# Nine blocks at a time for the narrow products of a layer: a group size in a graph kernel's last stage

## The chip, the cores and the metric

The kernel runs on one core of a Trainium2 chip. The metric is device time in microseconds: three runs of the kernel before took 556.18, 557.09 and 557.86 us, so its time is the median, 557.09.

## The reference

Four graph layers run one after another over x (3327 nodes of 64 features) with one dense matrix adj, whose entries are zero or positive. After each layer comes x = layernorm(x + layer(x)). Only the last layer matters here, and of it this core:

```python
support = input @ weight
mask = (adj != 0).astype(support.dtype)
rank = jnp.cumsum(mask, axis=1)
deg = rank[:, -1:]
k = jnp.minimum(deg, float(MAX_NEIGH))        # MAX_NEIGH = 100
pos = rank - (deg - k)
w = mask * jnp.where(pos > 0, DECAY ** (k - pos), 0.0)   # DECAY = 0.5
out = w @ support + bias
```

For every node, its neighbours are counted from the last column back. The last neighbour has weight 1, the one before it 1/2, and so on, up to a hundred of them. The output is the weighted sum of the neighbours' support rows.

## The kernel before

The matrix comes transposed and padded to 3328 = 26 blocks of 128 rows (`NB`), in HBM as `in_adjT`; a block's rows are the neighbours and its columns the nodes. Layer 1 goes through it once, layer 2 twice, and layer 3 once more. Everything in layer 3 is in `layers`, from line 523 on.

Layer 3 splits the nodes into two halves of 1664 columns (`HALF`) and each half into two chunks (c = 0 and 1) of 832, which a matmul covers in two pieces (e = 0 and 1) of 416 (`CW`). A half goes through the 26 blocks from the last to the first, so there are 52 steps. For each step:

- `masks(q)`, line 324: the half block `ah` is loaded by a DMA on SyncE's queue (832 KB; the first four blocks of each half are in SBUF already, as `kept`), and VectorE turns it into a bf16 `mask` of zeros and ones (L341). There are four `ah` buffers and six masks. It is called with q + 3 (`AHEAD`).
- `advance(c, q)`, line 544: TensorE adds to the counts in PSUM (`cnt`, one accumulator for each chunk) with `count` (L526): first what is left of block q (matrix `rest`), then the running count within block q + 1 (matrix `tri`). The counts are prepared so that their integer value is the bit pattern of a bf16 weight: a larger count is a smaller power of two.
- `read(c, q)`, line 531: the counts are clamped at zero and written as int16 into a weight tile `w`, which is then used as bf16. ScalarE reads chunk 0 (L541), and VectorE chunk 1 (L539). A chunk's next counts overwrite the accumulator, so they wait for this.
- `products(q, c)`, line 714: TensorE multiplies the weights by the support rows. The support in fp32 is kept as three bf16 parts. The first two stand side by side in `s12`, 128 columns wide, and are multiplied at once (`high`, L722) into an accumulator `acc` of 128 partitions. The third part, `s3`, has 64 columns only; its products (L737) go into one half of the accumulator's partitions, the lower for e = 0 and the upper for e = 1.

The wide products of a step follow when its weights are there, three steps later (`LEAD`). The narrow ones are put on a list and are done for several blocks at once:

```python
later.append((q, c))
if not last:
    high(q, c)
if last or c and len(later) == 2 * GROUP:
    for ql, cl in later:
        if last and cl != c:
            continue
        for e in range(2):
            nc.tensor.matmul(acc[h, cl][e * D : (e + 1) * D, e, :], s3[...], ws[ql, cl][:, e, :], ...)
```

`last` is the last block of a half: there each chunk's list is emptied before its last wide product. So a weight tile must live until its group is through, and `read` takes it from a pool whose depth follows from the group:

```python
w = l3w.tile([P, 2, CW], BF16, tag=f"w{c}", bufs=LEAD + GROUP + 2, ...)
```

The order of instructions on TensorE, VectorE and ScalarE is written out by hand: what the program says is the order of the queue. The loop is this:

```python
for q in range(LEAD, len(steps) + LEAD + 1):
    turn = q == NB + LEAD
    read(0, q, False)
    if turn: first_out = half_out(0, sums_out(0))
    read(1, q, True)
    if with_step: with_step.pop(0)()
    masks(q + AHEAD)
    p = q - LEAD if q < NB + LEAD else q - LEAD - 1
    for c in range(2):
        if p and not turn: products(p, c)
        if q < len(steps): advance(c, q)
        ...
```

So in a step's TensorE queue stand: wide products of chunk 0, counts of chunk 0, wide products of chunk 1, then the group of narrow ones if it is due, then the counts of chunk 1. `with_step` holds nine pieces of work left from the start of the layer (making the parts of the support, L644 to L653, and scaling rows for later, L626), one for each of the steps q = 3 to 11; some are VectorE's, some ScalarE's and GpSimd's. `half_out` is the output of the first half: a bias (L752 on ScalarE, L753 on VectorE), 13 small products that bring it back to rows (L759), the sum with x (L794), squares (L795), their sums (L798), a reciprocal square root (L239 to L246 and L555), the scaling (L803) and two stores. It is drawn out over the steps q = 29 to 34. After the loop `last_out` does the same for the second half.

Of the kernel before, what the change touches and what calls it, by code (L numbers as in the profile page):

```python
# [63 lines left out]
CUBIC_PLUS = 2 * CUBIC_ROOT - 1  # L64
CUBIC_REST = 1.75705840270866
NEIGH = 100
GROUP = 3
LEAD = 3
AHEAD = 3
STEP = float(2**7)  # L70
# [6 lines left out]
def kernel(  # L77
# [234 lines left out]
    def layers(ctx, x2, x3, begun_here, kept, ready, ahead_ctx, strm):  # L312
# [218 lines left out]
        def read(c, q, vector):  # L531
            if q >= len(steps):
                return
            h, jb = steps[q]
            w = l3w.tile(
                [P, 2, CW], BF16, tag=f"w{c}", bufs=LEAD + GROUP + 2, name=f"w_{h}_{jb}_{c}"
            )
# [176 lines left out]
        def products(q, c):  # L714
# [5 lines left out]
            def high(q, c):  # L720
                for e in range(2):
                    nc.tensor.matmul(  # L722
                        acc[h, c][:, e, :], s12[:, slot(jb)].rearrange("p t d -> p (t d)"),
                        ws[q, c][:, e, :], start=first, stop=last,
                    )
# [4 lines left out]
# [4 lines that stand above are left out]
# [1138 lines left out]
```

## Time and profile before

| | |
|---|---|
| median of three runs | 557.09 us |
| the profiled execution, its time | 557.54 us |
| its span, first to last instruction | 555.7 us |
| TensorE (PE) busy | 527.5 us, 95% |
| VectorE (DVE) busy | 372.2 us, 67% |
| ScalarE (ACT) busy | 276.8 us, 50% |
| GpSimd (POOL) busy | 207.4 us, 37% |
| mean granted TensorE clock | 0.979, and 1.00 in layer 3's loop |
| L526, counts, 408 matmuls 128 x 128 x 416 | 339 to 340 ns each |
| L722, wide products, 208 matmuls 128 x 128 x 416 | 339 ns each |
| L737, narrow products, 208 matmuls 128 x 64 x 416 | 344 ns each, 22.1 us busy |
| L539, VectorE's read of counts, 49 | 1023 ns each |
| L541, ScalarE's read of counts, 55 | 863 ns each |
| L341, masks from `ah`, 42 | 1034 ns each |
| `ah` loads, 832 KB each, 42 | 6.3 us from issue to landing |

A matmul's length in the table is that from its start to its end; matmuls overlap, and what counts is how far apart they start. "Idle before" is time in which an engine stood still ahead of an instruction, with the one that ended it behind the arrow; "issue" means that nothing in the profile explains it. The busy share of TensorE is an average over layers with different limits, so the prediction cuts the span into stretches. In layer 3's loop the profile is best read step by step, by the starts of instructions on the timeline.

### The profile page before, as it was taken

To read this page: it belongs to the slowest core of one execution; us is meant where nothing else is said; L and a number is where in the kernel's file an instruction comes from. 1 tells how busy PE (TensorE), PEld (TensorE's weight loads), DVE (VectorE), ACT (ScalarE), POOL (GpSimd) and SP (SyncE) were. 2 spreads that over 40 slices of the span, in tenths; PEclk is the share of its full clock that TensorE was granted. 3 is DMA by queue.
4 is the path that set the end of the run, shared out by engine and by line. 5 is a ranking of instruction groups with operands and counts; after the bars stand their busy time and mean duration, and the time that the engine had idled before them with its cause. 6 is when DMAs were issued, how large, how long until landed. Compare 5 with 4: busy or idle time off the path is not lost.

```text
span 555.7 us, 7392 instructions
## 1 busy us (share of the span) xinstructions
PE 527.5 (95%) x2841; PEld 226.9 (41%) x2841; DVE 372.2 (67%) x549; ACT 276.8 (50%) x325; POOL 207.4 (37%) x85
## 2 busy tenths in 40 slices
PE   8799989999999999999999999999999999999991
PEld 5422222222222222964444444434455555545541
DVE  6799999999999999798000011200678877887733
ACT  4899999999999997620000100000464333433321
POOL 3699999999999999000000000000001000000000
PEclk9889999999999999799999999999999999999996
DMA  8958866666667536799998049999029994799601
GB/s 282 365 205 288 257 209 225 210 223 220 225 232 243 187 123 247 277 416 425 423 427 367 1 163 424 426 426 399 6 66 344 329 326 167 246 296 349 247 1 38
DMA packets 33893, 143.57 MB, mean 258 GB/s; under 512 B 10269, under 2 KB 11959, under 8 KB 28855
## 3 DMA queue, kind: packets, MB, share of 16 engines
q1 hardware_dynamic: 31511, 142.40, 69.7%
q10 hardware_dynamic: 2336, 0.59, 0.5%
q8 instruction: 24, 0.39, 0.3%
q14 instruction: 22, 0.18, 0.1%
HBM read 141.53 MB, written 0.87 MB: 256 GB/s over the span
## 4 chain that ended last, share of the span: by engine, by line
PE 68%; DVE 17%; issue 7%; ACT 6%; POOL 1%; DVEq 0%; POOLq 0%; ACTq 0%
PE cnt L421 26%; PE cnt L526 11%; DVE v L1124 10%; PE pq L1103 9%; PE acc L722 6%; PE acc L1136 4%; PE acc L737 3%; ACT pq L1116 3%; ACT sg L1076 2%; DVE a L1115 2%; DVE w L539 1%; PE cnt L412 1%; DVE mask L341 1%; PE idle L928 1%; PE x_w L1455 1%
## 5 line engine op out<-in xcount | busy, mean ns | idle before, releaser
L1088 POOL TENSOR_TENSOR sg<-sg,at 128x1664 f32<-128x1664 f32 x44 | 163.7, 3738 | 3.7 <-ACT sg L1076 2.2
L1103 PE MATMUL pq<-riT,ljT 64*128 64x416 f32 x416 | 101.0, 564 | 11.6 <-DVE v L1124 7.9
L1116 ACT ACTIVATE pq<-pq,al,ga 128x832 f32<-128x832 f32 x104 | 104.6, 1012 | 12.1 <-DVE a L1115 12.0
L1115 DVE SCALAR_TENSOR_TENSOR a<-pq,sg 128x832 f32<-128x832 f32 x104 | 105.3, 1013 | 4.5 <-PE pq L1103 2.3
L1124 DVE SCALAR_TENSOR_TENSOR v<-pq,a 128x832 f32<-128x832 f32 x104 | 105.4, 1014 | 3.3 <-ACT pq L1116 2.2
L1136 PE MATMUL acc<-v,xv 128*64 128x416 f32 x416 | 96.0, 541 | 0.0
L1076 ACT ACTIVATE sg<-lb,rb 128x1664 f32<-128x1664 f32 (+1 forms) x53 | 87.3, 1649 | 0.0
L541 ACT ACTIVATE w<-cnt 128x832 int16<-128x832 f32 x55 | 47.3, 863 | 71.5 <-PE cnt L526 71.4
L421 PE MATMUL cnt<-at_l,lj 128*64 128x416 f32 x448 | 80.4, 513 | 0.0
L653 POOL TENSOR_TENSOR s<-sq,s 128x384 bf16<-128x384 f32 (+1 forms) x4 | 4.1, 1026 | 200.7 <-ACT s L652 200.7
L506 ACT ACTIVATE x<-cnt 128x416 f32<-128x416 f32 x8 | 4.1, 518 | 131.5 <-PE cnt L421 131.5
L539 DVE TENSOR_SCALAR w<-cnt 128x832 int16<-128x832 f32 x49 | 50.1, 1023 | 25.8 <-PE cnt L526 24.0
L1103 PEld LDWEIGHTS pq<-riT,ljT 64*128 64x128 f32 x416 | 31.7, 186 | 85.1 <-DVE v L1124 78.6
L526 PE MATMUL cnt<-mask,tri 128*128 128x416 bf16 x208 | 53.5, 339 | 0.1
L722 PE MATMUL acc<-w,s 128*128 128x416 bf16 x208 | 52.6, 339 | 0.5 <-DVE hid L794 0.5
L526 PE MATMUL cnt<-mask,rest 128*128 128x416 bf16 x200 | 51.6, 340 | 1.2 <-ACT w L541 0.6
L421 PEld LDWEIGHTS cnt<-at_l,lj 128*64 128x64 f32 x448 | 31.9, 137 | 46.2 <-issue 45.4
L1136 PEld LDWEIGHTS acc<-v,xv 128*64 128x64 f32 x416 | 20.7, 135 | 61.5 <-issue 57.8
L409 DVE COPY lj<-pn_l 128x512 f32<-128x512 f32 (+1 forms) x4 | 2.4, 592 | 61.6 <-PE pn_l L373 61.6
L341 DVE TENSOR_SCALAR mask<-ah 128x1664 bf16<-128x1664 f32 x42 | 43.4, 1034 | 0.0
L421 PE MATMUL cnt<-kept,lj 128*64 128x416 f32 x224 | 41.2, 513 | 0.0
L586 DVE TENSOR_TENSOR x<-x,xc 128x416 f32<-128x416 f32 x4 | 2.4, 588 | 41.5 <-ACT x L506 41.5
(285 smaller groups left out, 441.9 us busy)
## 6 DMA issues: line engine op xcount, KB each, us to landing
at_l<-in_adjT SPq DMA_DIRECT2D x24, 1664.0 KB, 12.8
at<-in_adjT SPq DMA_DIRECT2D x44, 832.0 KB, 4.9
ah<-in_adjT SPq DMA_DIRECT2D x42, 832.0 KB, 6.3
bt_l<-in_adjT SPq DMA_DIRECT2D x8, 1664.0 KB, 14.9
kept<-in_adjT SPq DMA_DIRECT2D x7, 1664.0 KB, 8.1
lb<-lf_rows SPq DMA_DIRECT2D x2, 384.0 KB, 6.1
ljT<-ljT SPq DMA_DIRECT2D x4, 128.0 KB, 5.5
x<-in_x ACTq DMA_DIRECT2D x1, 416.0 KB, 5.4
```

Source lines behind the costliest of these rows:

```text
L341: nc.vector.tensor_scalar(mask[q], at, 0.0, None, ALU.not_equal)
L421: nc.tensor.matmul(acc[c][h * D : (h + 1) * D, :], hw[:, slot(jb), :], blocks[jb][:, o : o + CW], start=c not in begun, stop=last, skip_gr ...
L526: nc.tensor.matmul(cnt[c][:, e, :], mat, mask[q][:, of], start=start, stop=(mat is tri), skip_group_check=True,)
L539: nc.vector.tensor_scalar(w.bitcast(I16), cnt[c], 0.0, None, ALU.max)
L722: nc.tensor.matmul(acc[h, c][:, e, :], s12[:, slot(jb)].rearrange("p t d -> p (t d)"), ws[q, c][:, e, :], start=first, stop=last,)
L1076: nc.scalar.activation(sg[:, :, of], lbs[:, :, of], AF.Sigmoid, bias=rb[:, sl : sl + 1])
L1088: nc.gpsimd.tensor_tensor(sg[:, :, of], sg[:, :, of], at[:, :, of], ALU.mult)
L1103: nc.tensor.matmul(pq[:, h, :], ljT[h != jb // NBH][rows, of], riT[rows, ch * CW : (ch + 1) * CW], start=True, stop=True,)
L1115: stt(a_s[t], pqs[t], CUBIC_PLUS, us.pop(t), op0=ALU.add, op1=ALU.mult)
L1116: nc.scalar.activation(pqs[t], pqs[t], AF.Square, bias=al[:, one], scale=ga[:, one])
L1124: stt(w, pqs.pop(t), CUBIC_REST, a_s.pop(t), op0=ALU.add, op1=ALU.mult)
L1136: nc.tensor.matmul(accs[cp, ci][h * D : (h + 1) * D, :], xv[:, slot(jb), :], w[:, h, :], start=(jb == orders[cp][0]), stop=(jb == orders[c ...
```

## The change

The group size of the narrow products goes from three blocks to nine.

```diff
-GROUP = 3
+GROUP = 9
 LEAD = 3
 AHEAD = 3
```

By `len(later) == 2 * GROUP` the narrow products are now taken up after nine blocks, 36 matmuls in a row where there were 12. In each half of 26 blocks the groups end after the 9th and the 18th block, and the other eight blocks stand at the half's end, 16 matmuls for each chunk, ahead of its last wide product. By `bufs=LEAD + GROUP + 2` each chunk's pool of weight tiles has 14 buffers where it had 8. No other line of the kernel changes; the number of instructions on every engine stays the same.

## The prediction

> **What bounds the kernel now.** The change touches layer 3 alone, so I first cut the span: layer 3 runs from the first counting matmul at 397.6 us to the end at 555.7. The chain that ended last gives the whole:
>
> ```profile
> PE 68%; DVE 17%; issue 7%; ACT 6%; POOL 1%; DVEq 0%; POOLq 0%; ACTq 0%
> ```
>
> Shares of the span cannot say which engine decides in which step, so I read the timeline of TensorE over an undisturbed stretch. Columns: start, length, engine and line, shapes, count.
>
> ```profile
> 445.38 0.52 PE L526 MATMUL cnt<-mask,rest 128*128 128x416 bf16 x2
> 445.74 0.52 PE L526 MATMUL cnt<-mask,tri 128*128 128x416 bf16 x2
> 446.09 0.52 PE L722 MATMUL acc<-w,s 128*128 128x416 bf16 x2
> 446.53 1.25 PE L737 MATMUL acc<-w,s 128*64 128x416 bf16 x12
> 447.71 0.53 PE L526 MATMUL cnt<-mask,rest 128*128 128x416 bf16 x2
> ```
>
> Full-width pairs start 0.352 us apart (0.176 a matmul), with no gap. A step is six such pairs, 2.11 us. The third part (L737, 64 columns wide) comes in groups of twelve matmuls; groups start 7.61 us apart here (438.92, 446.53), which leaves 7.61 - 3 x 2.11 = 1.28 us for a group. Its twelve matmuls run as six concurrent pairs, 6 x 0.176 = 1.06, so **0.22 us a group is neither**: 0.09 lost on the way in (446.53 where 446.44 was due), the rest on the way out. The view of line 737 shows where it sits, and how many groups there are: the weight loads stand idle in front of it 20 times, 6.9 us, by "issue".
>
> The same stretch on VectorE:
>
> ```profile
> 443.12 1.02 DVE L539 TENSOR_SCALAR w<-cnt 128x832 int16<-128x832 f32 x1 [0.15 <-PE cnt L526]
> 444.06 1.02 DVE L341 TENSOR_SCALAR mask<-ah 128x1664 bf16<-128x1664 f32 x1
> 445.23 1.02 DVE L539 TENSOR_SCALAR w<-cnt 128x832 int16<-128x832 f32 x1 [0.15 <-PE cnt L526]
> ```
>
> A step without a group costs it 0.94 + 1.02 = 1.96 us, of 2.11: **0.15 us to spare**. A group gives it 1.28 more. Where VectorE has other work it decides. The chain in order of time (start, length, what) through the output of the first half shows it:
>
> ```profile
> 484.26 1.02 DVE mask L341
> 485.28 0.20 DVE v_out L798
> 485.48 0.31 issue
> 485.79 0.48 DVE v_out L798
> 486.27 0.93 DVE w L539
> 487.20 0.93 DVE mask L341
> 488.14 0.09 DVE v_out L555
> ...
> 490.51 0.93 DVE mask L341
> 491.44 0.60 DVE hid L803
> 492.04 0.94 DVE w L539
> 492.99 0.04 issue
> 493.03 0.86 PE cnt L526 x4
> ```
>
> From 484.26 to 493.03 no matmul is on it, though TensorE's timeline has a group of L737 at 486.74: that group is free today.
>
> **What the Trainium skill says.** "TensorEngine Tiling (Array Packing)", Tiling Modes: changing the tiling mode drains TensorE, and column tiles work in parallel. The trace agrees on both: 0.22 us a group, and twelve narrow matmuls in the time of six. "TensorE: Matmul & The Clock Gate", Architectural detail, calls VectorE's queue strict FIFO: a late mask holds the read of counts behind it. "SBUF — State Buffer", two separate sides: a VectorE operation in a two-port mode and GpSimd exclude each other. Here the mask at 411.18, begun beside GpSimd's L653 (411.10, 0.91 us), took 1.72 us against 1.02.
>
> **The change, part by part.** No instruction is added or dropped; the build of the changed kernel keeps every engine's count, and orders TensorE anew. q is the loop's step, p the block multiplied: p = q - 3 in the first half, q - 4 in the second.
>
> 1. *Switches saved.* Before, each half has groups after p = 2, 5, ..., 23 of that half, and two at its end (one for each column chunk): 10, and 20 in all as seen. After: p = 8, 17 and the two at the end: 4, and 8. Twelve fewer, 12 x 0.225 = **-2.70 us**. The 208 narrow matmuls themselves only move: a group taken out brings all behind it 1.28 forward, and 1.06 of it comes back in a later group. That holds where TensorE decides; below, each place that loses a group is priced by the stall it leaves.
>
> 2. *First steps, q = 5 to 10.* VectorE has other work here (L648 0.55 and 0.68; L626 0.55 and 0.68), and the groups at q = 5 and 8 go. At q = 6, VectorE's order (read 414.78, L648, mask 416.19) puts the next read at 417.14 and its end at 418.16; matmuls need it at 418.10 and hear of it 0.05 later: 0.11 late. At q = 8 the L648 of 0.68 gives, by the same sum, a read that ends at 424.72 for a matmul due at 424.54: 0.23. L626 at q = 10 and 11 falls under the group that stays at q = 11. Together **+0.34**. GpSimd's L653 can stretch a mask once: 0 to +0.7, taken as nothing, since the masks then start near its end.
>
> 3. *q = 26.* The first block of the second half has no "rest" pairs, so its step is 0.70 shorter and VectorE is behind: a stall of 0.23 today (467.04 where 466.81 was due), and a second one when the group at 468.88 is gone: VectorE's read starts at 467.83 straight behind a mask and is heard of at 467.83 + 1.02 + 0.05 = 468.90, the matmuls are due at 468.44 + 0.35 = 468.79: **+0.11**.
>
> 4. *Output of the first half, q = 30 to 34.* Without the group at q = 32 the matmuls would be due at 486.65, but the read ends at 487.21; then ScalarE's read waits behind the square root (488.25), which waits for VectorE, and at q = 33 the matmuls start at 490.56, as today. The 1.28 us saved are lost whole. At q = 35 the matmuls are due at 495.13 and the read ends at 495.25, seen at 495.30: 0.17. Together **+1.45**. From there VectorE has no other work.
>
> 5. *Loads of the adjacency, between groups.* SyncE issues a load when the mask four earlier has ended. Between groups that leaves 4 x 2.11 - 1.02 = 7.42 us to land, where today a group or two lies between (8.7 or more). Landing took 4.7 to 10.9 us, median 6.3; around 506 to 516 us:
>
> ```profile
> DMA to landing us min/median/max: 6.3/7.6/7.9
> ```
>
> Loads issued less than four steps ahead of a group, or under it, land in its shadow (3.4 us). Left are the last four of each eight-step run, q = 16 to 19 and 43 to 46. With today's times only the second run is late, by 7.9 - 7.4 = 0.5; rate makes it worse: a load of 832 KB (851,968 bytes) each 2.11 us asks 404 GB/s, where 498 to 505.6 us moved 369, one load each 2.31, with the DMA engines at share 1.00. Bounds: 0, and 1.6: if each of four loads adds 0.2 to the queue, the second run is 1.3 late, and 0.3 is kept for the first (6.6 us at most around 440). I take **+0.50**, what today's times give. Queued behind a late mask: VectorE's next read, and TensorE behind that.
>
> 6. *The tail.* The last products of the second chunk become eight blocks in place of two, so ScalarE's L752 (540.41, 0.96 us) ends under them; L759 starts behind the last product, 541.13, and not at 541.42: **-0.29**.
>
> 7. *Nothing:* the twelve buffers, six for each chunk (1664 bytes a partition each). They move addresses: the first mask load waits for VectorE and TensorE instead of a DMA and TensorE, with 27 us in hand (issued 377.17, used 411.18). A read finds its buffer free two steps early (14 deep, oldest released after p = 8, needed at p = 14). In a 3.4 us group ScalarE and VectorE run dry, but the next counts need only reads that are already done.
>
> Sum: -2.70 - 0.29 + 0.34 + 0.11 + 1.45 + 0.50 = -0.59. The profiled execution took 557.54 us (span 555.7 and 1.8 around it), 0.45 above the median of 557.09; the sum goes on the median: **556.5 us**.
>
> **The rivals.**
> - *TensorE decides throughout, faster:* items 1 and 6 with 2 and 3 only, -2.54: 554.6. It needs VectorE to catch up in the output steps, as it does after 495 us. Against: the chain above. Partial forms (loads never late, 0.3 less in item 4) reach 555.7.
> - *Masks starve, slower:* loads are served no faster than today's average, one each 2.54 us. Then each of the two long runs loses 8 x (2.54 - 2.11) less about 1.0 of slack, 2.4; two are 4.8 in place of 0.5: 560.8. It decides from landing times of 7.4 us on; the two runs must lose 2.8 for a slowdown past 0.3%. For it: 7.6 around 511 us. Against: 369 GB/s were reached, and there is no VectorE wait on a load today.
> - *The change does nothing:* the groups would stay short. The build's order shows TensorE without L737 until nine blocks are through, so this is open only if a long group's switches cost 2.5 times a short one's; that undoes item 1: +2.1, 559.2.
>
> **How the numbers follow.** About 0.3% (1.7 us) is what a measurement can tell from none. Balance 0.63 (own range 555.6 to 558.0), faster 0.20, slower 0.17, the last with the unpriced waits in it. The range 554.8 to 558.7 leaves a tenth out on each side.
>
> **What would show it.** Right: eight groups of L737, full ones of 36 matmuls in about 3.4 us; "issue" idle of its loads near 2.7; a chain through VectorE from q = 31 to 35; L759 right behind the last product. Wrong: VectorE idle by a load of ah, or masks over 1.1 us; TensorE stalls at q = 12 to 20 or 39 to 46; a group costing other than 0.22 beyond its pairs.

## The result, and the profile after

The changed kernel takes 555.70 us (median of 20 runs) against 557.24 of the kernel before (20 runs), a ratio of 0.9976 (95% interval 0.9967 to 0.9985): 0.8 to 1.8 us shorter. The middle of that, 1.3 us, is within the 0.3% that the prediction called no difference, on the side that it forecast.

A whole run scatters by more than the pieces discussed here; what is ahead of layer 3 is the same code in all kernels of this study, and ends up to 2 us apart from one execution to the next. So I use one more measure, the **loop time**: from the count that waits 0.25 us for ScalarE at the start of layer 3 (406.41 us before, 406.21 after) to the first L759 behind the loop (541.42 and 540.07). It is 135.01 us before and 133.86 after: **-1.15 us**. A loop time comes from the one profiled execution of its kernel; how well it repeats is seen below, where a kernel with the same order of work (e_bufs) comes within 0.01 us of before.

The view of line 737, after; what weight loads waited for, us and times:

```profile
  issue: 2.7, 8
```

Eight groups, 0.34 us in front of each, where there were 20 and 6.9. TensorE's timeline around a full group, after:

```profile
428.42 0.51 PE L722 MATMUL acc<-w,s 128*128 128x416 bf16 x2
428.87 3.35 PE L737 MATMUL acc<-w,s 128*64 128x416 bf16 x36
432.15 0.53 PE L526 MATMUL cnt<-mask,rest 128*128 128x416 bf16 x2
```

From 428.77, where the next pair was due, to 432.15 are 3.38 us: 18 x 0.176 and 0.21. A long group pays its way in and out once, as a short one does.

The chain in order of time, after, over the output of the first half:

```profile
484.66 0.48 DVE v_out L798
485.14 0.93 DVE w L539
486.07 0.93 DVE mask L341
...
490.90 0.94 DVE w L539
491.85 0.04 issue
491.89 0.86 PE cnt L526 x4
```

VectorE's pieces have their old lengths. The group at 486.74 is gone, and the counts still start where VectorE lets them. TensorE's timeline, after, has the two waits that took the group's place (q = 32 and 33). A **stall** below is how much later than 0.176 us after the matmul before it a matmul starts; the idle time in brackets is 0.16 us less, because it counts only from that matmul's end:

```profile
486.12 0.51 PE L526 MATMUL cnt<-mask,rest 128*128 128x416 bf16 x2 [0.44 <-DVE w L539]
...
488.13 0.51 PE L526 MATMUL cnt<-mask,rest 128*128 128x416 bf16 x2 [0.80 <-ACT w L541]
```

The loads issued from 506 to 516 us, the window shown in the prediction, after:

```profile
DMA to landing us min/median/max: 5.7/6.3/6.3
```

They are faster than before (6.3/7.6/7.9), not slower. And those issued from 439 to 446 us, the last four before the next long group in the first half:

```profile
DMA to landing us min/median/max: 6.6/6.7/6.8
```

VectorE's timeline, after, has its only wait for a load in the loop, in front of the first of these two:

```profile
500.91 1.03 DVE L341 TENSOR_SCALAR mask<-ah 128x1664 bf16<-128x1664 f32 x1 [0.61 <-DMA ah<-in_adjT]
504.78 1.02 DVE L539 TENSOR_SCALAR w<-cnt 128x832 int16<-128x832 f32 x1 [2.84 <-PE cnt L526]
```

It falls under the long group that starts at 500.57: VectorE stands 2.84 us more before TensorE gives it new counts, and TensorE has no stall there.

### The profile page after: what moved, and what is told of

Read it like the earlier page. It is cut to its first block, busy times and chain, and to the rows that moved or that the text cites. A ratio compares the mean times of both kernels' runs of the same rounds, so it can differ in the third digit from the quotient of the medians.

```text
span 554.4 us, 7384 instructions
## 1 busy us (share of the span) xinstructions
PE 524.2 (95%) x2841; PEld 227.4 (41%) x2841; DVE 371.9 (67%) x549; ACT 276.6 (50%) x325; POOL 207.5 (37%) x85
## 4 chain that ended last, share of the span: by engine, by line
PE 64%; DVE 18%; ACT 9%; issue 7%; DVEq 0%; POOL 0%; ACTq 0%; POOLq 0%
PE cnt L421 26%; PE cnt L526 11%; DVE v L1124 10%; PE pq L1103 7%; PE acc L722 6%; ACT pq L1116 4%; ACT sg L1076 4%; PE acc L737 3%; PE acc L1136 3%; DVE a L1115 2%; DVE w L539 1%; DVE mask L341 1%; PE cnt L412 1%; PE idle L928 1%; PE pn_l L373 1%
## 5 line engine op out<-in xcount | busy, mean ns | idle before, releaser
L653 POOL TENSOR_TENSOR s<-sq,s 128x384 bf16<-128x384 f32 (+1 forms) x4 | 4.1, 1027 | 198.0 <-ACT s L652 198.0
L1088 POOL TENSOR_TENSOR sg<-sg,kept 128x1664 f32<-128x1664 f32 (+1 forms) x10 | 30.0, 3028 | 0.8 <-ACT sg L1076 0.8
```

The lines of the kernel that those rows point to most:

```text
L1088: nc.gpsimd.tensor_tensor(sg[:, :, of], sg[:, :, of], at[:, :, of], ALU.mult)
```

## The experiments

Theory: each group less is worth 0.22 us, and each place that lost one gives back what VectorE is late there. All of it in one table; "loop" is the loop time less that of before, and the ratio is of whole runs to those of before. e_wide computes something else and ran once, so it has no ratio.

| run | groups of L737 | loop, us | whole runs | ratio (95% interval) |
|---|---|---|---|---|
| after | 8 | -1.15 | 20 | 0.9976 (0.9967 to 0.9985) |
| e_bufs | 20 | -0.01 | 22 | 0.9994 (0.9983 to 1.0005) |
| e_first | 14 | -0.92 | 5 | 0.9967 (0.9955 to 0.9980) |
| e_second | 14 | -0.19 | 14 | 0.9987 (0.9976 to 0.9999) |
| e_six | 12 | +0.04 | 22 | 1.0007 (0.9996 to 1.0018) |
| e_one | 54 | +6.30 | 4 | 1.0088 (1.0066 to 1.0110) |
| e_wide | 20, of full width | +12.97 | 1 | none; 570.05 us |
| e_ah3_3 | 20 | +0.19 | 12 | 1.0004 (0.9991 to 1.0017) |
| e_ah3_9 | 8 | +4.18 | 5 | 1.0052 (1.0026 to 1.0078) |
| e_out | 9 | -2.19 | 5 | 0.9943 (0.9930 to 0.9956) |
| e_best | 10 | -2.29 | 6 | 0.9947 (0.9926 to 0.9968) |
| e_best5 | 10 | -2.55 | 16 | 0.9967 (0.9954 to 0.9981) |

Three intervals do not hold their loop's difference (e_first, e_one, e_out). They come from four or five runs, and runs of one kernel lie up to 3.5 us apart (before), so small steps are read from the loop.

**Buffers alone.**

```diff
-[P, 2, CW], BF16, tag=f"w{c}", bufs=LEAD + GROUP + 2, ...
+[P, 2, CW], BF16, tag=f"w{c}", bufs=LEAD + 9 + 2, ...          # GROUP stays 3
```

> Groups of three as before, with the 14 weight buffers a chunk of the changed kernel: only depth and addresses move. Theory (the groups alone matter): 0 against before, within 0.3, and layer 3's length within 0.1 us of before's. Rival (depth or addresses give the gain): -1.3 us.

Nothing moved, in the loop or in whole runs. The gain is not in the depth or the addresses.

**One half at a time.**

```diff
-if last or c and len(later) == 2 * GROUP:
+if last or c and len(later) == 2 * (3 if h else GROUP):     # e_first
+if last or c and len(later) == 2 * (GROUP if h else 3):     # e_second
```

> Groups of nine in the first half only; the second half keeps three, and both chunks keep 14 weight buffers. Theory (0.225 us for each group less, minus the stalls VectorE then makes): 14 groups of L737, 6 fewer than before, -1.35, plus stalls of 0.10, 0.23 and 0.11 at q = 6, 9 and 26: -0.9 us against before, and the output steps q = 30 to 35 as before, with its group at q = 32 free. Rival (the gain comes from the deeper weight pool and moved addresses): -1.3 us here and in the run with nine in the second half alone, and a TensorE time line that gains outside the group starts.

> Groups of three in the first half, of nine in the second only, 14 weight buffers. Theory: 14 groups, -1.35, the tail -0.28, and the output steps lose +1.45 (stalls of about 0.6 at q = 32, 0.7 more than before at q = 33 and 0.16 at q = 35): -0.2 us against before. Rival (TensorE decides throughout, VectorE catches up in the output steps): -1.6. Rival (deeper pool and addresses): -1.3.

Both came out at the theory's sums: -0.92 and -0.19 in the loop. The stalls in the traces are those named: 0.10, 0.23 and 0.11 us in the one; 0.60 at q = 32, 0.96 at q = 33 (0.28 before) and 0.16 at q = 35 in the other. Six groups are gone in each half, 1.35 us; the first half keeps two thirds of that, the second nearly nothing, though the shorter tail (0.28) is in its sum. The deeper-pool rival, the same gain in both, falls.

**A group size in between.**

```diff
-GROUP = 9
+GROUP = 6
```

> Groups of six, 11 weight buffers. Theory (count the groups, then the stalls where they were taken away): 12 groups, 8 fewer than before, -1.81; the output steps lose their group at q = 32 but keep one at q = 35, +1.28; the first steps keep groups at q = 8 and 14 but not at 5 and 11, so L626 at q = 10 and 11 makes TensorE wait, +0.10 and +0.48; q = 26 keeps its group; the tail gains nothing, two blocks as before: +0.05 us against before, so no gain though 8 groups are gone. Rival (each saved group is worth 0.225, wherever it stood): -1.8.

+0.04 us in the loop: eight groups fewer than before, and no gain at all. The stalls are those summed: 0.10 at q = 6, 0.10 and 0.36 behind VectorE's L626 of q = 10 and 11, for which 0.48 was summed, and those of q = 32 and 33. So a count of groups does not give the time; nine differs from six in where its groups fall too (q = 11 covers L626) and in the tail.

**The price of a group.**

```diff
-GROUP = 9
+GROUP = 1
```

> A group after every block: 54 groups of L737 where there were 20, six weight buffers a chunk. Theory (0.225 us for each group, whatever its length): 34 x 0.225 = 7.65 more, of which about 0.45 falls into the output steps where VectorE decides and about 0.7 into stalls that stand in the first steps and at q = 26: +6.5 us against before, from 6.0 to 7.2. Rival (the loss grows with the group, or hides behind a short one): under +4.

+6.30 in the loop. 34 more groups are 7.65; the stalls that stood in the first steps, at q = 26 and in the output steps shrink by 1.4, since groups now fall there, and the tail is 0.17 longer: 6.4 by this sum. One group of a single block, on TensorE's timeline of this run:

```profile
441.82 0.52 PE L722 MATMUL acc<-w,s 128*128 128x416 bf16 x2
442.26 0.54 PE L737 MATMUL acc<-w,s 128*64 128x416 bf16 x4
442.74 0.53 PE L526 MATMUL cnt<-mask,rest 128*128 128x416 bf16 x2
```

From 442.17, where the next pair was due, to 442.74 are 0.57 us: 2 x 0.176 and 0.22. So the price does not depend on the length: it is 0.21 to 0.22 for 1, 3 and 9 blocks. Whole runs say +3.7 to +6.1, a little less than the loop.

**What the price is.**

```diff
-acc[h, cl][e * D : (e + 1) * D, e, :], s3[:, slot(steps[ql][1]), :],
+acc[h, cl][:, e, :], s12[:, slot(steps[ql][1])].rearrange("p t d -> p (t d)"),
```

> Groups of three as before, but the narrow products are replaced by the wide weights of the same block into the same accumulator (128 columns, not 64), so the third part of the support is left out and the first two are added once more. The tiling of the array never changes in the loop. Theory (the 0.225 us is the change of the tiling): a group of twelve costs 12 x 0.176 = 2.11 us and nothing more, its neighbours start 0.176 after and before it, and the issue idle of its weight loads is gone. Rival (the loss comes from changing accumulator, weights or order): 2.33 us a group.

TensorE's timeline of this run:

```profile
440.59 0.52 PE L722 MATMUL acc<-w,s 128*128 128x416 bf16 x2
440.94 2.27 PE L737 MATMUL acc<-w,s 128*128 128x416 bf16 x12
443.05 0.52 PE L526 MATMUL cnt<-mask,rest 128*128 128x416 bf16 x2
```

Twelve full-width matmuls take 2.11 us and start 0.35 after the pair before them, without a gap on either side, and line 737's loads have no idle time left. The group's place, its number of matmuls and its accumulator are those of before, and its weights still change with each block. So the 0.22 us comes with the narrow width, in and out, and not with the change of accumulator or order. That it is the draining which the Trainium skill names for a change of tiling ("TensorEngine Tiling (Array Packing)", Tiling Modes) fits; the run takes away all that is narrow at once, and can't tell the draining from it.

**Fewer buffers for the loads.**

```diff
-at = l3w.tile([P, HALF], F32, tag="ah", bufs=4, ...)
+at = l3w.tile([P, HALF], F32, tag="ah", bufs=3, ...)          # e_ah3_9 with GROUP = 9, e_ah3_3 with GROUP = 3
```

> Groups of nine with three buffers for the adjacency's half blocks in place of four. Between groups a load then has 3 x 2.11 - 1.02 = 5.3 us to land, and loads took 4.4 to 7.9. Theory (landing time against the steps between groups decides whether masks starve): VectorE waits for loads in the eight-step runs, 1 to 4 us of TensorE stalls, +2.5 against groups of nine with four buffers, so about +1.2 against before. Rival (loads have slack to spare): no change against groups of nine, -1.3 against before.

> Groups of three, with three buffers for the adjacency's half blocks in place of four. Each three steps hold a group, so a load has 3 x 2.11 + 1.28 - 1.02 = 6.6 us to land, more than most take. Theory: 0 to +0.8 us against before, far less than the same cut costs with groups of nine. Rival (the cut costs by itself, by the number of loads in flight): as much here as there.

With groups of three the cut costs 0.19 us in the loop; with groups of nine 5.33 (from -1.15 to +4.18). VectorE waits for a load eight times in both, 6.9 and 9.7 us in all; the short groups cover nearly all of it. VectorE's timeline of e_ah3_9, two masks:

```profile
440.78 1.03 DVE L341 TENSOR_SCALAR mask<-ah 128x1664 bf16<-128x1664 f32 x1 [1.11 <-DMA ah<-in_adjT]
...
448.75 1.03 DVE L341 TENSOR_SCALAR mask<-ah 128x1664 bf16<-128x1664 f32 x1 [1.92 <-DMA ah<-in_adjT]
```

So masks can starve, as in the slower rival, and long groups sharpen it. With four buffers it is not far away: in the run after, the tightest mask of the eight-step runs starts at 446.67, 0.59 us after its load has landed. I had summed 1 to 4 us, and it is more: the loads that the late masks of the eight-step runs waited for took 6.2 to 6.8 us, where 5.3 were given, though fewer were in flight.

**The free group given back.** One more group of blocks 26 to 28, at q = 32:

```diff
-if last or c and len(later) == 2 * GROUP:
+if last or c and (len(later) == 2 * GROUP or q == NB + 2):     # q is the block's place here; NB + 2 = 28 is read at step 32
```

> Groups of nine, and one more group of three blocks (26 to 28) at q = 32, in the output steps where VectorE decides. Theory: that group is free again, as it was before: TensorE's stalls at q = 32 and 33 fall from 1.56 to about 0.5, 1.06 us of narrow products leave the later groups, so -1.1 us against groups of nine alone, and -2.4 against before. Nine groups in all, the issue idle of L737's weight loads about 3.1 us. Rival (the output steps are bounded by the reads' latency on TensorE's own side, a group there costs its full 1.28): +0.2 against groups of nine.

TensorE's timeline of this run:

```profile
485.15 0.52 PE L722 MATMUL acc<-w,s 128*128 128x416 bf16 x2
485.59 1.25 PE L737 MATMUL acc<-w,s 128*64 128x416 bf16 x12
486.77 0.53 PE L526 MATMUL cnt<-mask,rest 128*128 128x416 bf16 x2
...
488.12 0.51 PE L526 MATMUL cnt<-mask,rest 128*128 128x416 bf16 x2
```

Set this next to the two waits of the run after: the group fills them, and at q = 33 the counts start at 488.12 as they did at 488.13. Its 1.06 us of products are out of the later groups: the loop is 1.04 shorter than after's (-2.19 against -1.15).

**A second one, and a fifth load buffer.** e_best adds a group of one block at q = 33 (`q in (NB + 2, NB + 3)`); e_best5 has besides five `ah` buffers and 13 weight buffers a chunk.

> As the run with the extra group of three at q = 32, and one more of a single block at q = 33. Theory: the single block costs 0.35 + 0.22 = 0.58 where the stalls of q = 33 and 34 (0.24 and 0.36) leave room for it, so 0.35 more is saved: -1.4 against groups of nine alone, -2.8 against before; ten groups. Rival (each change of the tiling costs where it stands): no better than the run with one extra group, or 0.2 worse.

> As the run with extra groups at q = 32 and 33, with five buffers for the adjacency's half blocks in place of four (and 13 weight buffers a chunk[...]). In the run with four, VectorE waited once for a load, 0.53 us, where no group covered it, and TensorE stood 0.25. Theory: the load behind the stores is issued a step earlier, the wait and the 0.25 go, -0.25 in layer 3 against that run, -2.5 against before; 13 weight buffers cost at most 0.1 a group. Rival (more loads in flight only slow each other, or 13 buffers hold the reads up): the same or up to 0.5 longer.

The second group brought 0.10, not 0.35, and whole runs do not tell it from the run with one. The stalls it was to fill are gone, but VectorE's timeline of e_best shows a new wait, and TensorE stood 0.25 us behind it:

```profile
500.57 1.03 DVE L341 TENSOR_SCALAR mask<-ah 128x1664 bf16<-128x1664 f32 x1 [0.53 <-DMA ah<-in_adjT]
501.51 1.02 DVE L539 TENSOR_SCALAR w<-cnt 128x832 int16<-128x832 f32 x1
502.65 1.03 DVE L341 TENSOR_SCALAR mask<-ah 128x1664 bf16<-128x1664 f32 x1
```

It is the load that fell under a long group in the kernel after, the one that SyncE issues behind the output's two stores; the groups have moved, and the cover with them. With five buffers the wait is gone and the loop is 0.26 shorter, as summed. By the loop e_best5 is the fastest. Whole runs put all three ahead of before, but do not follow the loop in their order: e_out comes out at 0.9943 and e_best5 at 0.9967, with intervals that hardly overlap, and e_best5's just reaches its loop's -2.55 us. A part of that lies outside the profiled span: what a run takes beyond its span is 2.06 us on average in e_best5 and 1.75 in before. This was not followed up, so which of the three is fastest stays open.

## Why the prediction was right

It gave 556.5 us from a median of 557.09, -0.59; measured -1.54 in medians, -1.15 in the loop. The range of 554.8 to 558.7 held, but it is wide: it would have held no change at all. The change itself came out about twice as large as forecast (0.59 lies outside the measured 0.8 to 1.8 us), and the median of 555.70 is only just inside the prediction's own range, 555.6 to 558.0. Part by part:

1. *Switches, -2.70:* right. Twelve groups fewer, 0.21 to 0.22 each at every length.
2. *First steps, +0.34:* stalls of 0.10 and 0.23, at q = 6 and, behind the L648 of q = 8, at q = 9. GpSimd's L653 (423.51, 1.15 us) ran beside the start of a mask at 424.42, which took 1.13 us and cost TensorE nothing.
3. *q = 26, +0.11:* 0.11.
4. *Output of the first half, +1.45:* 0.60 + 0.68 + 0.16 = 1.44. e_second and e_out show it from both sides.
5. *Loads, +0.50:* **wrong, 0.** This is the term that failed: "I take +0.50, what today's times give". Today's times did not carry over to the new spacing. The last four loads before the next long group, which have 7.42 us to land, took 6.6 to 6.8 us in the first half and 5.7 to 6.3 in the second. The slow times belong to the spacing of before: the load for step 48 (issued at 511 in before) took 7.6 us in before, e_bufs and e_first, which have groups of three in the second half, and 6.3 and 6.6 in after and e_second, which have groups of nine there. What is new is that the queue runs down at a long group: no load is issued from 430.38 to 435.05 nor from 501.97 to 506.76, and the DMA engines' share falls to 0.24 (435 to 436 us) and 0.29 (506 to 507); before, it is 0.84 or more in every us from 506 to 512. That the loads behind it are faster for this reason is likely, not shown. Nor was 369 GB/s a limit: in e_best the masks that run right behind their loads start 2.04 to 2.08 us apart (500.57, 502.65, then 504.69), some 413 GB/s, faster than the steps.
6. *Tail, -0.29:* right. L759 starts at 540.07, right behind the last product; 0.28.

Without item 5 the sum is -1.09, and the loop says -1.15. Two of the prediction's signs of being wrong appeared, VectorE's wait for a load (0.61 us) and a mask over 1.1 us; neither reached TensorE. The faster rival (VectorE catches up) is refuted by item 4, but its partial form "loads never late" is what happened. The slower one is right that masks can starve, with three buffers or where no group covers the step of the stores, but not by its rate of one load each 2.54 us: at the end of the first half's run they landed at 446.08, 448.11, 450.18 and 452.17. That the change might do nothing is refuted by the full group's 3.38 us.

## What to carry to other kernels

Ask of a batched piece of work not only what each batch costs, but which engine decides at the place where it stands: a batch that fills another engine's wait is free, and to take it away saves nothing. A fixed cost for each change of tiling is saved by batching only where TensorE decides; so batch there, and leave a small batch in each place where TensorE would wait, with an eye on what the later batches then no longer cover. And landing times are taken under the queue's present load: when a change moves the pauses between loads, they have to be measured again, as here, where 7.6 us became 6.3.

## What the runs showed of the hardware

In layer 3 of these runs a load of 832 KB landed in 4.3 to 6.4 us where no other load was in flight when it was issued, and in 6 to 8 with three in flight; with the queue full they landed, at best, some 2.0 us apart. That the price of narrow groups between full-width matmuls is the same for 4, 12 and 36 of them, 0.21 to 0.22 us in and out together, was expected from one length alone.
